# Eight rows of an expert product and a recurrence on one Trainium2 core: first-group weight sums through PSUM or put off, and a rewritten ending in quarters of 32 partitions

## The chip, the cores and the metric

The kernel runs on one core of one Trainium2 chip. A core has five engines that run their own queues of instructions: TensorE (PE; its weight loads are shown apart as PEld), VectorE (DVE), ScalarE (ACT), GpSimd (POOL) and SyncE (SP), which here issues the transfers. Work is passed between them by semaphores. SBUF and PSUM are the on-chip memories, both of 128 partitions; TensorE writes to PSUM only, in banks of 2 KB a partition (512 float32 columns). The metric is the device time of one execution in microseconds; lower is better.

## What is computed

The input x has 4 x 1024 tokens of width 1024, all in float32. Cut to what matters:

```python
xn  = layernorm(x)
# recurrence, batch 0 is enough (see below)
g   = sigmoid(xn @ gate_w.T + gate_b);  u_g = xn * g
d_eff = d + mean_over_tokens(u_g) @ d_lr_u @ d_lr_v / 4
s   = ...                       # first-order recurrence along the tokens, with a, b
y   = c * s + d_eff * u_g
# experts: indices are expert numbers 0..7, and they index rows of the output
p   = softmax(xn @ wr.T);  top 2 -> indices, gates
h   = silu(silu(xn @ w1.T) @ w3.T) @ w2.T
moe = zeros;  moe[indices[:, k]] += gates[:, k] * h      # k = 0, 1
out = x + y * silu(moe)
```

The scatter adds into rows 0 to 7 only, since there are eight experts. All other rows of moe are zero, silu(0) is zero, and these rows of the output are those of x. So the kernel copies x to out for all rows past the eighth, and computes eight rows: the sum over all 4096 tokens, C.T @ h2 with h2 = silu(silu(xn w1.T) w3.T) and C the 4096 x 8 matrix of gates, then (C.T @ h2) @ w2.T, then the last line. The gate g is needed for all tokens of batch 0, because of the mean; the recurrence is needed for eight tokens.

## The kernel before

**Groups and products.** The tokens are taken in four groups of 1024 (`sb` 0 to 3). For each group there are two 1024 x 1024 x 1024 products, `u` (xn with w1) and `m` (the result with w3); group 0 has a third, `g` (xn with gate_w), interleaved with `u`. Each is done with Strassen-Winograd's seven products in place of eight (`order` gives their order, by number 1 to 7) of 512 x 512 x 512, and each of those again with seven of 256 x 256 x 256, except some called plain, which use eight. A small product is four matmuls of 128 x 128 weights and 256 columns (`small`); the profile counts two records for each, so eight a small product. `Half` is one 512-product: `step(n)` issues its small product n, into the PSUM banks X, Z and Y, and drains them by `first` and `more`, on VectorE or ScalarE.

**The sums.** Strassen-Winograd needs sums of the operands' blocks. On the token side these are `s1` to `s4` (blocks) and `left_sums` (quarters of blocks); on the weight side the blocks 4 to 7 are differences of blocks of the weight (in `first_weights` for w1 and gate_w: `five`, `six`, `seven`, `four`; in `first_w3`: `take`), and `fresh_sums` and `t_sum` make four quarters of each (GpSimd). A block is 128 x 2048 values in SBUF, in four parts of 512 columns, so 1 MB; a quarter is 256 KB. There are 20 blocks and 18 quarters, handed out in turn. Group 0 makes the weight-side sums and stores them in HBM (`keep_block`, `keep_quarter`); groups 1 to 3 load them (`load_kept`, `load_kept_sum`). Plain products need no quarters, so group 0 makes those of w1 product 1 only to be kept (`kept_sums_1`), and group 1 makes those of w3 products 2 and 7 afresh.

**The order of the work.** `at(place, f)` puts a piece of work at a place of a written-out order; a small product of one half takes two places, and two halves overlap, so that a half adds 7 places (a plain one 8). `start[kind, sb, i]` is the place at which a product begins, END the place of the end. The loop over `steps` runs what is due and then the next small product. A generator's `yield n` puts its rest n places later. All instructions issued through `pe`, `dve`, `act`, `pool` and `sync` (all shown as L89, the line of the recording helper) stay in that order on their engine. SyncE's queue is in order too: a load behind a store that waits for its data waits as well.

**The other work that the change meets.** `stats` loads the rows of the next group and ScalarE sums them; `norm` normalizes the next group; `recurrence` makes y, [128, 8, 8] (width in 8 parts, 8 tokens).

**The end.** As soon as the two h2 blocks (I, 0) and (I, 1) of one token half I are complete, `scatter` issues eight matmuls of 32 weight columns (gates, padded from 8 to 32 columns) into the bank `acc`: column group g = 2 J + n % 2, so that the output's four sets of 32 partitions hold the two width halves J and, of each, two partial sums. The bank stays open over the whole program. The last `scatter` comes after the last product. Then the bank is copied, eight matmuls with `selh` (a selecting matrix) turn and add it to `ta`, 16 matmuls with w2 give `pp` in two banks, in four partial sums of 32 partitions each; for each half of 512 columns `pp` is copied, added up by a matmul with `sel` into 8 partitions, and goes through Silu, multiplication by y, addition of x and a store:

```python
    for n in range(2):
        cols = slice(n * H, (n + 1) * H)
        nc.vector.tensor_copy(ppS[:, cols], pp[n])
        ps = ps_x.tile([E, H], F32, tag="X", name=f"p2_{n}")
        nc.tensor.matmul(ps, sel, ppS[:, cols], start=True, stop=True)
        nc.scalar.activation(o8[:, cols], ps, AF.Silu)
        nc.vector.tensor_mul(o8[:, cols], o8[:, cols], y8[:, cols])
        nc.vector.tensor_add(o8[:, cols], o8[:, cols], x8[:, cols])
        nc.sync.dma_start(out[0:E, cols], o8[:, cols])
```

Of the kernel before, what the change touches and what calls it, by code (L numbers as in the profile page):

```python
# [22 lines left out]
def kernel(  # L23
# [113 lines left out]
    def quarter(uses=1):  # L137
# [13 lines left out]
    sel = const.tile([P, E], F32, tag="sel", name="sel")  # L151

    selh = const.tile([P, 2, E], F32, tag="selh", name="selh")
    nc.gpsimd.memset(selh, 0.0)
# [4 lines left out]
        sel, ident.rearrange("p (g e) -> p e g", e=CG)[:, 0:E, :], AX.X, ALU.add  # L159
    )  # L160
    dve.tensor_copy(ids, ids_i)
    for h in range(2):
        dve.tensor_copy(selh[64 * h : 64 * h + 64, h, :], sel[64 * h : 64 * h + 64, :])
# [7 lines left out]
    y = const.tile([P, KD, E], F32, tag="y", name="y")  # L171
# [315 lines left out]
    def fresh_sums(kind, sb, i, t, keep):  # L487
# [3 lines left out]
        for j in range(4):  # L491
# [6 lines left out]
            op_ts[kind, sb, i, j] = o  # L498
            if keep:
                at(start[kind, sb, i] + 2 * T_AT[j], keep_quarter, name, i, j, o)  # L500
# [4 lines left out]
    def sub(eng, out, p, q, n=4):  # L505

        for h in range(0, 4, 4 // n):
            eng.tensor_tensor(
                out[:, h : h + 4 // n], p[:, h : h + 4 // n], q[:, h : h + 4 // n], ALU.subtract
            )  # L510
            yield 0.5

    def load_kept(kind, sb, i, fresh):
        name = {"u": "w1", "m": "w3"}[kind]
        t = block(1 + fresh)
        sync.dma_start(t.tile, weights[name][raw[i]] if i in raw else kept[name, i])
        op_t[kind, sb, i] = t
# [6 lines left out]
    def first_weights(kind, name, before=()):  # L524
# [15 lines left out]
        def kept_sums_1():  # L540
            s = []
            for j in range(4):
                o = quarter(1 + (j < 2))
                t_sum(o, b[1], s, j)
                s.append(o)
                if j == 1:
                    s[0].drop()
                if j == 3:
                    s[1].drop()
                at(S(1) + 18 + 3 * j, keep_quarter, name, 1, j, o)  # L550
                yield 3
            b[1].drop()

# [10 lines left out]
        def six():  # L564
            yield from sub(dve, b[6], b[6], b[5])
# [13 lines left out]
        def four():  # L579
            yield from sub(pool, b[4], b[4], b[6])  # L580
# [9 lines left out]
        load(1, (0, 0), 2 + keep, before)  # L590
        one()
        if keep:
            at(S(1) + 8, kept_sums_1)
# [12 lines left out]
        for i in order["u"][1:]:  # L606
            if kind == "g" and i in PLAIN_G:
# [4 lines left out]
                lambda i=i: fresh_sums(kind, 0, i, op_t[kind, 0, i], keep),  # L612
            )

    def first_w3():
# [10 lines left out]
        def take(i, p=None, q=None):  # L626

            if p is not None:
                for h in range(4):
                    dve.tensor_tensor(b[i][:, h], b[p][:, h], b[q][:, h], ALU.subtract)  # L630
                    yield 1
# [15 lines left out]
        at(S(1) - 20, take, 5, 5, 1)  # L647
        at(S(1) - 12, take, 6, 6, 5)
# [633 lines left out]
```

## Time and profile before

| what | us |
|---|---|
| median of 3 runs | 851.44 (850.01 to 852.07) |
| the profiled execution | 850.65 |
| its span, first to last instruction | 848.6 |
| TensorE busy in the span | 831.2 |
| VectorE busy | 565.7 |
| GpSimd busy | 496.6 |
| ScalarE busy | 234.5 |
| mean granted TensorE clock | 0.997 of full |

The profile is of one execution; its times begin at the first instruction. A row of the timeline has the start, the length, the engine, the line, the operation, output and inputs by tile name, the shape, and in brackets how long the engine stood before it and who released it. A row of the groups has a count, the total busy time and the mean of one in nanoseconds. A row of the busy times by stretch has, for each engine, busy microseconds and the number of instructions that touch the stretch, then the granted clock, the share of the DMA engines in use, and GB/s. Matmuls overlap, so a busy TensorE is not one at its peak.

### The profile page before, as it was taken

What the parts mean: (1) busy time and instruction counts of PE and PEld (TensorE: products, weight loads), DVE (VectorE), ACT (ScalarE), POOL (GpSimd) and SP (SyncE); (2) the same over time, 40 slices, a digit from 0 to 9 for tenths busy, and PEclk for the clock granted to TensorE, in tenths of its full rate; (3) what the DMA queues carried; (4) which work ended last, traced back from release to release, by engine and by line L of the source; (5) the groups of instructions that cost most, each with busy time, mean ns of one, the idle gap of its engine ahead of it and who ended that gap; (6) DMA issues with size and microseconds to landing.
All of it is one profiled execution on the core that took longest, in us unless ns stands there. A gap on an engine that the chain in (4) does not pass through costs nothing.

```text
span 848.6 us, 11192 instructions
## 1 busy us (share of the span) xinstructions
PE 831.2 (98%) x4103; PEld 701.9 (83%) x4103; DVE 565.7 (67%) x889; ACT 234.5 (28%) x375; POOL 496.6 (59%) x375
## 2 busy tenths in 40 slices
PE   7999999989999999999999999999999999999997
PEld 6886888878888868888888778888888688888882
DVE  6989796988699425575897225775993246546642
ACT  0212213776121207343012226531122021220121
POOL 0389999995628764436866753753449444465400
PEclk9999999999999999999999999999999999999998
DMA  8953447631976877529976757659775455555600
GB/s 335 421 193 131 161 169 273 260 124 51 361 303 216 305 268 255 200 87 343 363 234 242 266 183 267 234 190 398 270 246 183 165 192 209 195 192 191 264 0 2
DMA packets 54013, 189.71 MB, mean 224 GB/s; under 512 B 6140, under 2 KB 9388, under 8 KB 42312
## 3 DMA queue, kind: packets, MB, share of 16 engines
q1 hardware_dynamic: 53960, 189.01, 60.2%
q8 instruction: 33, 0.54, 0.3%
q14 instruction: 20, 0.16, 0.1%
HBM read 165.86 MB, written 39.87 MB: 242 GB/s over the span
## 4 chain that ended last, share of the span: by engine, by line
PE 87%; DVE 7%; DMA 4%; SPq 1%; issue 1%; ACT 0%; DVEq 0%; ACTq 0%
PE X_u L89 21%; PE X_m L89 20%; PE Z_u L89 11%; PE Z_m L89 11%; DVE b L89 7%; PE Y_u L89 5%; PE X_g L89 5%; PE Y_m L89 4%; PE Z_g L89 3%; DMA b<-in_xT 3%; PE acc L89 2%; PE plT L89 2%; DMA b<-in_gw 1%; SPq L89 1%; PE Y_g L89 1%
## 5 line engine op out<-in xcount | busy, mean ns | idle before, releaser
L89 POOL TENSOR_TENSOR q<-b 128x512 f32<-128x512 f32 x144 | 202.8, 1421 | 230.6 <-DVE b L89 51.8
L89 ACT ACTIVATE b<-b 128x512 f32<-128x512 f32 (+1 forms) x152 | 105.0, 695 | 331.2 <-DVE b L89 322.1
L89 DVE TENSOR_TENSOR b<-b,b 128x512 f32<-128x512 f32 x176 | 181.8, 1052 | 3.3 <-POOL q L89 0.5
L89 POOL TENSOR_TENSOR q<-b,q 128x512 f32<-128x512 f32 x91 | 132.1, 1454 | 5.7 <-issue 3.3
L89 POOL TENSOR_TENSOR b<-b,b 128x512 f32<-128x512 f32 x72 | 94.5, 1336 | 40.5 <-PE X_u L89 34.4
L89 DVE TENSOR_TENSOR b<-X_u,b 128x512 f32<-128x512 f32 x87 | 59.9, 689 | 71.4 <-PE X_u L89 70.8
L89 PE MATMUL X_u<-q,q 128*128 128x256 f32 x432 | 103.1, 381 | 0.9 <-DVE b L89 0.9
L89 DVE TENSOR_TENSOR b<-X_m,b 128x512 f32<-128x512 f32 x84 | 57.2, 687 | 62.3 <-PE X_m L89 61.0
L89 PE MATMUL X_m<-q,q 128*128 128x256 f32 x416 | 98.3, 379 | 0.0
L89 PEld LDWEIGHTS X_u<-q,q 128*128 128x128 f32 x432 | 81.1, 190 | 16.1 <-issue 3.0
L89 POOL TENSOR_TENSOR q<-q,b 128x512 f32<-128x512 f32 x53 | 72.5, 1368 | 30.3 <-PE X_u L89 26.2
L89 PEld LDWEIGHTS X_m<-q,q 128*128 128x128 f32 x416 | 79.0, 190 | 10.8
L89 DVE TENSOR_TENSOR b<-b,bc 128x1024 f32<-128x1024 f32 (+1 forms) x62 | 72.8, 1178 | 3.6 <-ACT bc L89 2.5
L89 PE MATMUL X_m<-b,b 128*128 128x256 f32 x272 | 63.7, 380 | 0.9 <-DVE b L89 0.9
L89 PE MATMUL X_u<-b,b 128*128 128x256 f32 x248 | 58.8, 381 | 5.7 <-DVE b L89 5.5
L89 PEld LDWEIGHTS X_m<-b,b 128*128 128x128 f32 x272 | 51.3, 190 | 8.9 <-DVE b L89 1.9
L89 PEld LDWEIGHTS X_u<-b,b 128*128 128x128 f32 x248 | 46.8, 190 | 13.5 <-DVE b L89 6.7
L89 DVE TENSOR_TENSOR b<-Z_u,b 128x512 f32<-128x512 f32 x47 | 32.4, 689 | 28.6 <-PE Z_u L89 28.0
L89 PE MATMUL X_u<-b,q 128*128 128x256 f32 x216 | 51.3, 380 | 0.0
L89 PE MATMUL Y_u<-b,b 128*128 128x256 f32 x216 | 51.3, 380 | 0.0
L89 PE MATMUL Z_u<-q,b 128*128 128x256 f32 x216 | 51.3, 380 | 0.0
L89 DVE TENSOR_TENSOR b<-Z_m,b 128x512 f32<-128x512 f32 x48 | 32.8, 686 | 27.5 <-PE Z_m L89 26.1
(143 smaller groups left out, 1171.5 us busy)
## 6 DMA issues: line engine op xcount, KB each, us to landing
q<-w SPq DMA_DIRECT2D x160, 256.0 KB, 3.3
b<-in_w SPq DMA_DIRECT2D x35, 1024.0 KB, 7.4
b<-w_T SPq DMA_DIRECT2D x24, 1024.0 KB, 5.1
b<-in_xT SPq DMA_DIRECT2D x15, 1024.0 KB, 9.5
w<-q SPq DMA_DIRECT2D x56, 256.0 KB, 5.6
b<-in_x SPq DMA_DIRECT2D x12, 1024.0 KB, 7.3
w_T<-b SPq DMA_DIRECT2D x8, 1024.0 KB, 4.1
b<-in_gw SPq DMA_DIRECT2D x7, 1024.0 KB, 10.2
```

What stands on the lines that cost most here:

```text
L89: r = f(*args, **kwargs)
```

## The change

In group 0 the differences `six` and `four` of w1 and gate_w (sums of SBUF operands on VectorE and on GpSimd) are made by `with_bank`: ScalarE copies one operand, quarter by quarter, to one of two PSUM banks (`acc` and the bank of `rows`), and VectorE subtracts it from there. The quarters to be kept of w1 product 1 are no longer made in group 0's first stage, but by `late_sums` in its w3 stage, from a block that is read again; those of w3 products 2 and 7 are made by `late_sums` in group 1's u stage, so that group 1's m stage loads them as every other. In `first_w3`, takes 7 and 4 go to GpSimd, and takes 5 and 6 begin two places later.

At the end the scatter of the last group is cut in three: blocks (0,0) and (1,1) shortly after the last product has begun, (1,0) before its last but one small product, and the last block, (0,1), in a bank of its own, `accB`, in two halves. The rest of the sum is transposed and added in the meantime (`most`); `the_rest` then runs the product with w2 in pieces, as parts of its left side come in. The result is made as four quarters of 256 columns on 32 partitions each, with y and x laid out in the same way by `rows` 40 places before the end, and stored with four transfers from two queues.

```diff
-    selh = const.tile([P, 2, E], F32, tag="selh", name="selh")
-    nc.gpsimd.memset(selh, 0.0)
-    y = const.tile([P, KD, E], F32, tag="y", name="y")
+    y = const.tile([P, KD, CG], F32, tag="y", name="y")
+    pool.memset(y, 0.0)
...
+    def with_bank(out, p, q):
+        def copy(j):
+            spare[0] += 1
+            ps = acc if spare[0] % 2 else ps_acc.tile([P, H], F32, tag="rows", name="spare")
+            act.copy(ps, q[:, j])
+            return ps
+        ps = copy(0)
+        yield 0.5
+        for j in range(4):
+            ahead = copy(j + 1) if j < 3 else None
+            dve.tensor_tensor(out[:, j], p[:, j], ps, ALU.subtract)
+            ps = ahead
+            yield 0.5
+    def late_sums(name, i):
+        t = block()
+        sync.dma_start(t.tile, weights[name][raw[i]] if i in raw else kept[name, i])
+        yield 5
+        s = []
+        for j in range(4):
+            o = quarter(1 + (j < 2))
+            t_sum(o, t, s, j)
...
+            yield 2.5
+            keep_quarter(name, i, j, o)
+        t.drop()
...
-        def kept_sums_1():
...
         def six():
-            yield from sub(dve, b[6], b[6], b[5])
+            yield from with_bank(b[6], b[6], b[5])
...
         def four():
-            yield from sub(pool, b[4], b[4], b[6])
+            yield from with_bank(b[4], b[4], b[6])
...
         def take(i, p=None, q=None):
-                for h in range(4):
-                    dve.tensor_tensor(b[i][:, h], b[p][:, h], b[q][:, h], ALU.subtract)
-                    yield 1
+                yield from sub(pool if i in (7, 4) else dve, b[i], b[p], b[q], 4, 1)
...
-        at(S(1) - 20, take, 5, 5, 1)
-        at(S(1) - 12, take, 6, 6, 5)
+        at(S(1) - 18, take, 5, 5, 1)
+        at(S(1) - 10, take, 6, 6, 5)
...
-            fresh = kind == "m" and sb == 1 and i in PLAIN_M
-            at(S - (12 if fresh else 10), load_kept, kind, sb, i, fresh)
-            if fresh:
-                at(
-                    S - 5,
-                    lambda i=i: fresh_sums("m", 1, i, op_t["m", 1, i], True),
-                )
-            for j in range(0 if fresh else 4):
+            at(S - 10, load_kept, kind, sb, i)
+            for j in range(4):
                 at(S + 2 * T_AT[j] - 9, load_kept_sum, kind, sb, i, j)
...
+    at(start["m", 0, 1] + 14, late_sums, "w1", 1)
+    for n, i in enumerate(PLAIN_M):
+        at(start["u", 1, 1] + 4 + 14 * n, late_sums, "w3", i)
...
+    def rows():
+        end = block()
+        yR, xR = end[:, 0, 0:Q], end[:, 0, Q : 2 * Q]
+        pool.memset(xR, 0.0)
+        for w in range(4):
+            sync.dma_start(xR[CG * w : CG * w + E, :], x[0:E, w * Q : (w + 1) * Q])
+        yield 2
+        ty = ps_sm.tile([P, 2, P], F32, tag="sm", name="ty")
+        for j in range(2):
+            for w in range(4):
+                pe.matmul(ty[CG * w : CG * (w + 1), j, :], y[:, 2 * w + j, :], ident, ...)
+        yield 1
+        dve.tensor_copy(yR, ty.rearrange("e j p -> e (j p)"))
...
+    def most():
+        accs = fin["accs"]
+        act.copy(accs[:, Q:H], acc[:, Q:H])
+        dve.tensor_copy(accs[:, 0:Q], acc[:, 0:Q])
+        yield 2
+        tT = ps_sm.tile([P, 4, P], F32, tag="sm", name="tT")
+        for k in range(4):
+            pe.transpose(tT[:, k, :], accs[:, k * P : (k + 1) * P], ident)
+        yield 1
+        half = fin["half"] = fin["half"].rearrange("p (k e) -> p k e", e=E)
+        for J, o in ((0, fin["accT"][:, 0:4, 0:E]), (1, half)):
+            dve.tensor_copy(o, tT[:, :, 64 * J : 64 * J + E])
+            dve.tensor_add(o, o, tT[:, :, 64 * J + CG : 64 * J + CG + E])
+    def part_out(ks, start, stop):
+        for g, k in enumerate(ks):
+            for n in range(2):
+                r = (g + 2 * n) % 4 * CG
+                pe.matmul(fin["p"][n][r : r + CG, :], fin["accT"][:, k, :],
+                    w2_sb[n, k // 4][:, k % 4, :], ...)
+    def the_rest():
...
+        def last_block(b):
+            for n in range(4):
+                a, mt = n // 2, n % 2
+                pe.matmul(accB[n * CG : (n + 1) * CG, b * Q : (b + 1) * Q],
+                    gates[NS - 1][:, n, :], c[:, 2 * a + b, mt * Q : (mt + 1) * Q], ...)
+        last_block(1)
+        dve.tensor_copy(accBs[:, Q:H], accB[:, Q:H])
+        part_out(range(4), True, False)
+        ta = ps_sm.tile([P, 4, E], F32, tag="sm", name="ta")
+        for b in (1, 0):
+            ks = slice(2 * b, 2 * b + 2)
+            if b == 0:
+                dve.tensor_copy(accBs[:, 0:Q], accB[:, 0:Q])
+            for k in (2 * b, 2 * b + 1):
+                pe.matmul(ta[:, k, :], accBs[:, k * P : (k + 1) * P], sel[:, 0:E], ...)
+            if b == 1:
+                last_block(0)
+            dve.tensor_add(accT[:, 4 + 2 * b : 6 + 2 * b, 0:E], ta[:, ks, :], half[:, ks, :])
+            part_out((4 + 2 * b, 5 + 2 * b), False, b == 0)
+        for n, copy in ((0, dve.tensor_copy), (1, act.copy)):
+            copy(pp[:, n * H : (n + 1) * H], fin["p"][n])
+        p2 = ps_y.tile([P, Q], F32, tag="Y", name="p2")
+        for w in range(4):
+            pe.matmul(p2[CG * w : CG * (w + 1), :], sel, pp[:, w * Q : (w + 1) * Q], ...)
+        act.activation(o, p2, AF.Silu)
+        dve.tensor_mul(o, o, fin["y"])
+        dve.tensor_add(o, o, fin["x"])
+        for w in range(4):
+            (sync, act)[w % 2].dma_start(out[0:E, w * Q : (w + 1) * Q], o[CG * w : CG * w + E, :])
+    at(END - 40, rows)
+    at(start["m", NS - 1, 7] + 15, scatter, NS - 1, [(0, 0), (1, 1)])
+    at(END + 1.5, scatter, NS - 1, [(1, 0)])
+    at(END + 1.6, most)
+    at(END + 6, the_rest)
```

What is removed at the end is the old ending: the transposes of y to 8 partitions, the copies of `acc`, `ta`, `pp` and the loop quoted above.

## The prediction

> **What bounds the kernel now.** The page's busy table comes first. TensorE is busy for 98% of the span, so only time in which it stands, or the stretch after its last large product, can be won.
>
> ```profile
> PE 831.2 (98%) x4103; PEld 701.9 (83%) x4103; DVE 565.7 (67%) x889; ACT 234.5 (28%) x375; POOL 496.6 (59%) x375
> ```
>
> The timeline of TensorE alone shows where it stands (the bracket: idle time before, and who ended it). Past the first 17 us there are five holes; the fifth is 0.29 us at 368.39.
>
> ```profile
> 69.39 1.99 PE L89 MATMUL X_u<-b,b 128*128 128x256 f32 x8 [1.59 <-DVE b L89]
> ...
> 161.94 1.97 PE L89 MATMUL X_u<-q,q 128*128 128x256 f32 x8 [0.94 <-DVE b L89]
> ...
> 174.91 1.99 PE L89 MATMUL X_u<-b,b 128*128 128x256 f32 x8 [2.36 <-DVE b L89]
> ...
> 430.10 1.99 PE L89 MATMUL X_m<-b,b 128*128 128x256 f32 x8 [0.92 <-DVE b L89]
> ```
>
> Together 1.59 + 0.94 + 2.36 + 0.92 + 0.29 = 6.1 us. The first four end with VectorE, which drains the bank that the next product writes. The busy time by stretch (columns: PE, weight load, VectorE, ScalarE, GpSimd, clock, DMA share, GB/s) says why VectorE is late: in the first group GpSimd has no rest either.
>
> ```profile
> 67.00:102.00 35.00, 33.41 (x198) 26.20 (x197) 31.24 (x60) 9.50 (x17) 35.00 (x26) 1.00 0.38 143
> 102.00:150.00 48.00, 48.00 (x224) 42.27 (x223) 39.37 (x52) 11.20 (x19) 46.58 (x32) 1.00 0.62 234
> 150.00:186.00 36.00, 32.70 (x150) 28.17 (x150) 33.15 (x43) 26.54 (x37) 36.00 (x24) 1.00 0.46 179
> ```
>
> And the groups say what the two do to each other: one VectorE sum of two SBUF operands costs 1,052 ns in the mean, one with an operand in PSUM 689.
>
> ```profile
> L89 DVE TENSOR_TENSOR b<-b,b 128x512 f32<-128x512 f32 x176 | 181.8, 1052 | 3.3 <-POOL q L89 0.5
> ...
> L89 POOL TENSOR_TENSOR b<-b,b 128x512 f32<-128x512 f32 x72 | 94.5, 1336 | 40.5 <-PE X_u L89 34.4
> L89 DVE TENSOR_TENSOR b<-X_u,b 128x512 f32<-128x512 f32 x87 | 59.9, 689 | 71.4 <-PE X_u L89 70.8
> ```
>
> Last, the timeline of the end. The last large product is issued out at 830.77 (828.77 + 1.99), the span ends at 848.6: 17.8 us of chain.
>
> ```profile
> 828.77 1.99 PE L89 MATMUL X_m<-q,b 128*128 128x256 f32 x8
> ...
> 831.13 2.14 PE L89 MATMUL acc<-b,C 128*32 128x512 f32 x16
> ...
> 833.81 1.96 PE L1184 MATMUL ta<-selh,b 128*128 128x8 f32 x16 [0.54 <-DVE b L1177]
> ...
> 836.09 5.34 PE L1191 MATMUL pp<-b,accT 128*32 128x512 f32 x32 [0.32 <-DVE accT L1185]
> ...
> 842.35 0.59 ACT L1203 ACTIVATE b<-p 8x512 f32<-8x512 f32 x1 [8.14 <-PE p L1202]
> ...
> 845.00 0.68 DVE L1205 TENSOR_TENSOR b<-b,b 8x512 f32<-8x512 f32 x1
> ```
>
> **The change, part one: the first group.**
> (a) six, for u and g: 8 VectorE sums of SBUF operands become 8 ScalarE copies into PSUM and 8 sums from PSUM. In the timeline at 71.57 six such sums took 9.56 us, 1.59 each; at 0.69 each the eight give VectorE back 8 x 0.9 = 7 us. ScalarE's copy between SBUF and PSUM is 0.56 to 0.59 (the copies of X_u and bc); it has 25 of 35 us free there. Behind the copies in ScalarE's queue stands the drain of X_u of product 5, which TensorE needs before the bank's next use 8 us later; four copies ahead of it, two of them waiting for VectorE, cost about 2.5 us, so it is covered. Without that cover TensorE would stand for the 2.5.
> (b) four, for u and g: 8 GpSimd sums x 1.34 = 10.7 us leave an engine with 1.4 free us in 102 to 150; VectorE gains 8 x 0.69 = 5.5 us where it has 8.6 free, ScalarE 8 x 0.58 = 4.6 where it has 37.
> (c) The four sums kept of w1 product 1, and their four stores, leave the stretch 29 to 50 (4 x 1.27 = 5 us of GpSimd); everything behind them, the eight subtractions of five included, comes up to 5 us earlier. These matter: at 54.63 one VectorE sum took 5.34 us while GpSimd ran seven of them back to back, and the 1.59 us hole is the backlog from it. The sums come back at about 210 with one more 1 MB load.
> (d) In the w3 stage of the first group takes 7 and 4 go from VectorE to GpSimd (8 x 1.34), takes 5 and 6 start two places later, behind the drains that TensorE waits for at 162 and 175. With (c) GpSimd gets 12 sums, 16 us, in 186 to 292, where it is busy for 64 of 106.
> (e) w3 products 2 and 7: 8 sums and 8 stores move from about 395 to 430 to about 290 to 340, where VectorE is busy for only 37 of 78 us (stretch 292 to 370) and GpSimd for 46; in their old place come 8 loads of 256 KB. Two 1 MB blocks are read twice.
>
> A rule of the Trainium skill speaks against (a) and (b): "VectorE: DVE Perf Modes", section on the TRN2 errata, gives VectorE a fixed 120 cycles for a PSUM source against 58 for SBUF. By it each moved sum would cost 62 cycles at 0.96 GHz, 0.06 us, more: 16 x 0.06 = 1 us lost, and the copies on top. The rows say the reverse, 0.69 against 1.05 (1.59 at 71.57), since here GpSimd runs beside it. I take the rows.
>
> What of the holes goes: the 1.59 fully (c takes away more than its length); of 0.94 + 2.36 two thirds, 2.2, since GpSimd arrives there with about 10 us less behind it, but 24 of its sums remain there; of 0.92 half, because the chain that ended last shows the load of the next group's x (386.9 to 409) ahead of it, which stays; the 0.29 stays. That is 4.3 us. For the two places that receive work I charge 0.5 us of new holes: 3.8 net. Bounds: 6.1, all holes gone, and -2, the moved work making holes of its own.
>
> Behind waits: the loads of the x rows (four instead of one, on SyncE 40 places before the end) now wait for a memset on GpSimd, which stands up to 5.6 us for TensorE; late_sums' stores on SyncE wait for their GpSimd sum. Behind them in the queue stand the weight loads. Those are issued 9 or 10 places ahead, a place being 1.73 us (one step of 8 records), so 15.5 us, and land in 3.3: some 12 us of cover. If it is gone, the excess is a hole.
>
> **Part two: the end.** Ahead of the last product there now lie the scatter of (0,0) and (1,1) (as long as the old one, 1.85; it replaces the one at 826.92), the scatter of (1,0) alone, and four transposes. (1,0) uses two of the four column groups, so its 8 records take as long as 16 in four groups: 1.7. A transpose costs one 128-column weight load, 0.12 (ta: 16 in 1.96): 4 x 0.12 = 0.5 here. Their ACT and VectorE copies lie under the product in between (1.73 against about 1.1). The y products move off the end to 40 places ahead and stay near 0.43. So the last product is out at 830.77 + 2.2 = 833.0; I take 832.8. From there, with TensorE at 0.107 us a record of 512 columns in four groups (the fast part of pp), VectorE 0.42 for 128x256 (the copy of acc at L1177), 0.69 for 128x512, 0.06 for a hand-over:
>
> last_block(1) 0.43; part_out of four blocks, 16 records, 1.75 (the copy of accB, 0.75 to 1.17, lies beside it); ta 0.5; last_block(0) 0.43 (the add of 0.2 beside it); part_out, 8 records, 0.87; ta 0.5; add with hand-overs 0.35; part_out 0.87; copies of pp 0.75 (two engines); p2 0.6; Silu 0.45; multiply and add 2 x 0.42; issue and landing. Sum up to the issue: 0.43 + 1.75 + 0.5 + 0.43 + 0.87 + 0.5 + 0.35 + 0.87 + 0.75 + 0.6 + 0.45 + 0.84 = 8.3, with gaps 8.5. Before, from the last add's end (845.68) to the span's end lie 2.9 us. Now each of two queues issues two stores; one issue is 0.30 on SyncE, so 3.2. A ScalarE store is in no row; between SyncE's 0.30 and the 0.46 of SyncE's first loads (1.83 for four), near the first. End: 832.8 + 8.5 + 3.2 = 844.5, that is 4.1 us earlier.
>
> In this sum the clock is full. That is a choice. Before, the granted clock fell in the middle of pp:
>
> ```profile
> 836.00:836.50 0.50, 0.41 (x4) 0.16 (x8) 0.03 (x1) 0.00 (x0) 0.00 (x0) 0.99 0.00 0
> 836.50:837.00 0.50, 0.50 (x8) 0.21 (x4) 0.00 (x0) 0.00 (x0) 0.00 (x0) 0.50 0.00 0
> ...
> 840.00:841.00 1.00, 1.00 (x16) 0.31 (x9) 0.12 (x1) 0.00 (x0) 0.00 (x0) 1.00 0.00 0
> ```
>
> 3.2 us at half rate, 1.6 us lost. The skill's "TensorE: Matmul & The Clock Gate", section on the clock gate, halves the clock after an idle window of about 3.4 us. By that rule neither version should be halved, as TensorE never stood that long; by the row, three us of 8-column products and short gaps (833.3 to 836.1) were enough. The new end has no such stretch: about 60% of any 3.4 us is 256- or 512-column products. Were it halved from the second ta on, the last part_out and p2 would cost 1.3 more; from the start of the chain, with all its products (0.43 + 1.75 + 0.43 + 0.87 + 0.87 + 0.43), 4.8.
>
> **Sum.** 848.6 - 3.8 - 4.1 = 840.7 span; the profiled execution took 850.65, 2.05 more than its span, so 842.7. The median of the runs shown is 851.44, 0.8 above that execution; I say 843.0.
>
> **Rivals.**
> *Only one part delivers* (0.25): VectorE's 5.5 us from (b) and waits for ScalarE keep the holes, or the end is eaten by half clock and hand-overs. For it: VectorE is busy for 39 of 48 and 33 of 36 us and loses little in (b). Against: most of its excess is the 1.05 to 1.59 where 0.69 is the price. 850.65 - 4.1 or - 3.8, so 846.7, 847.3 by the median.
> *Nothing* (0.05): new holes as long as the old, and a halved end: 851.
> *Slower* (0.07): GpSimd becomes the bound in the w3 stage of the first group. Its 12 added sums are 16.2 us; its idle 42 of 106 us are waits for TensorE at fixed places, so if none of the sums fits in them, all delay TensorE: 850.65 - 8 + 16 = 859. It decides once half of them, 8 us, does. Against: at 97% GpSimd load (102 to 150) TensorE stood for nothing.
> *More* (0.08): all holes go: 840.5.
> The main case has 0.55. Its own range: 841 to 845.5. With the one-part case the range is 840 to 848.2; faster by over 0.3% (2.6 us, what a measurement of this kernel can tell) has 0.88, the same 0.05, slower 0.07.
>
> **What would show it.** Holes at 69, 162 and 175 gone and at 430 halved; GpSimd below 90% in 102 to 150; the sums from PSUM at 0.69; no hole over 0.5 us in 205 to 340; last product to span's end about 11.7 us at clock 1.00. Wrong if VectorE's drains still come late at 162 and 175, SyncE holds loads behind a store, or the clock is halved in part_out.

## The result, and the profile after

The changed kernel takes 842.43 us (median of six, 841.33 to 843.24), the kernel before beside it 850.57 (849.43 to 852.07): a ratio of 0.9899, with a 95% interval of 0.9885 to 0.9912. The profiled execution took 842.43 us, its span is 840.7 us, and its mean granted clock is 1.00. The forecast was 840.7 us of span and 843.0 of time.

The busy table of the page (busy us, share of the span, instructions):

```profile
PE 828.3 (99%) x4119; PEld 701.0 (83%) x4119; DVE 547.2 (65%) x890; ACT 243.2 (29%) x391; POOL 490.6 (58%) x377
```

TensorE's timeline (start, length; the bracket is the idle time before and who ended it). Past 17 us these are all the holes there are:

```profile
170.50 1.99 PE L89 MATMUL X_u<-b,b 128*128 128x256 f32 x8 [0.99 <-DVE b L89]
...
242.50 5.42 PE L89 MATMUL X_m<-b,b 128*128 128x256 f32 x24 [0.83 <-POOL b L89]
...
365.06 1.96 PE L89 MATMUL X_u<-b,b 128*128 128x256 f32 x8 [0.29 <-issue]
```

Before there were five, 6.1 us together. Those at 69, 162 and 430 are gone, the one at 175 went from 2.36 to 0.99, and there is a new one of 0.83 (the bracket names GpSimd; e7 below looks at what it waits for): 2.1 us now, 4.0 less.

The busy time by stretch, with the columns of before (TensorE, weight load, VectorE, ScalarE, GpSimd, clock, DMA share, GB/s):

```profile
67.00:102.00 35.00, 35.00 (x206) 27.92 (x205) 21.08 (x56) 14.05 (x26) 34.62 (x28) 1.00 0.57 204
102.00:150.00 48.00, 48.00 (x224) 42.25 (x223) 42.25 (x60) 17.18 (x29) 35.82 (x24) 1.00 0.56 209
150.00:186.00 36.00, 35.01 (x163) 30.50 (x162) 30.95 (x44) 25.90 (x36) 33.33 (x22) 1.00 0.41 159
205.00:245.00 40.00, 39.17 (x182) 34.18 (x182) 27.27 (x36) 6.17 (x10) 35.70 (x27) 1.00 0.92 355
```

VectorE is busy for 21.1 us in the first stretch where it was 31.2, GpSimd for 35.8 of 48 in the second where it was 46.6. The fourth row is where the late sums went. Before, GpSimd was busy there for 21.6 us and the DMA engines for 0.80 of the time; now it is 35.7 and 0.92. The row of before:

```profile
205.00:245.00 40.00, 40.00 (x187) 35.22 (x186) 30.65 (x43) 8.14 (x14) 21.61 (x15) 1.00 0.80 307
```

The groups of the page, and with them the rows that the view of the tile `spare` has for one of the two banks (there the durations are minimum, median and maximum in ns):

```profile
L89 DVE TENSOR_TENSOR b<-b,b 128x512 f32<-128x512 f32 x160 | 156.5, 995 | 2.9
...
L89 POOL TENSOR_TENSOR b<-b,b 128x512 f32<-128x512 f32 x72 | 95.4, 1352 | 35.8 <-PE X_u L89 26.4
```

```profile
L89 ACT COPY spare<-b x8: 575/590/595, 67.4 to 131.2; 128x512 f32<-128x512 f32 x8
...
L89 DVE TENSOR_TENSOR b<-b,spare x8: 675/678/689, 68.1 to 132.4; 128x512 f32<-128x512 f32 x8
```

A sum with one operand in PSUM takes 0.678 us with hardly any spread, also in the stretch from 67 to 102 us, where GpSimd is busy for 34.6 of 35. The VectorE sums that stay in SBUF still average 0.995.

The end, in the timeline of TensorE, ScalarE, VectorE and the queues:

```profile
822.79 1.91 PE L89 MATMUL acc<-b,C 128*32 128x512 f32 x8
...
826.90 1.89 PE L89 MATMUL X_m<-q,b 128*128 128x256 f32 x8
...
829.18 1.90 PE L89 MATMUL pp<-b,accT 128*32 128x512 f32 x16
...
833.86 1.06 PE L89 MATMUL pp<-b,accT 128*32 128x512 f32 x8 [0.27 <-DVE accT L89]
...
835.72 0.64 PE L89 MATMUL p<-b,sel 128*32 128x256 f32 x8 [0.80 <-DVE b L89]
...
836.84 0.88 DVE L89 TENSOR_TENSOR b<-b 128x256 f32<-128x256 f32 x2 [1.18 <-ACT b L89]
...
837.75 0.66 SPq L89 DMA_DIRECT2D out<-b  x2
837.75 0.96 ACTq L89 DMA_DIRECT2D out<-b  x2
```

The last large product is out at 826.90 + 1.89 = 828.79, and the span ends 11.9 us later; before it was 17.8. All products in it run at full clock; the clock is at half only from 840.2 on, when TensorE has nothing left to do. From the end of the last add (836.84 + 0.88 = 837.72) to the span's end lie 2.98 us.

### The profile page after: what moved, and what is told of

Its sections match the earlier page's. It is cut to its first block, busy times and chain, and to the rows that moved or that the text cites. A ratio compares the mean times of both kernels' runs of the same rounds, so it can differ in the third digit from the quotient of the medians.

```text
span 840.7 us, 11288 instructions
## 1 busy us (share of the span) xinstructions
PE 828.3 (99%) x4119; PEld 701.0 (83%) x4119; DVE 547.2 (65%) x890; ACT 243.2 (29%) x391; POOL 490.6 (58%) x377
## 4 chain that ended last, share of the span: by engine, by line
PE 91%; DMA 4%; POOL 1%; DVE 1%; issue 1%; SPq 1%; ACT 0%; POOLq 0%; DVEq 0%
PE X_u L89 23%; PE X_m L89 20%; PE Z_u L89 12%; PE Z_m L89 11%; PE Y_u L89 6%; PE X_g L89 6%; PE Y_m L89 5%; PE Z_g L89 4%; PE acc L89 2%; PE plT L89 2%; DMA b<-in_w 2%; DMA b<-in_gw 1%; DVE b L89 1%; DMA w<-q 1%; POOL q L89 1%
## 5 line engine op out<-in xcount | busy, mean ns | idle before, releaser
L89 POOL TENSOR_TENSOR q<-b 128x512 f32<-128x512 f32 x144 | 198.5, 1391 | 229.5 <-DVE b L89 51.4
L89 DVE TENSOR_TENSOR b<-b,b 128x512 f32<-128x512 f32 x160 | 156.5, 995 | 2.9
L89 POOL TENSOR_TENSOR q<-b,q 128x512 f32<-128x512 f32 x91 | 129.6, 1427 | 8.8 <-issue 6.7
L89 POOL TENSOR_TENSOR b<-b,b 128x512 f32<-128x512 f32 x72 | 95.4, 1352 | 35.8 <-PE X_u L89 26.4
L89 PEld LDWEIGHTS X_u<-q,q 128*128 128x128 f32 x432 | 81.3, 190 | 14.9 <-POOL q L89 1.7
L89 PEld LDWEIGHTS X_u<-b,b 128*128 128x128 f32 x248 | 46.9, 190 | 10.2 <-DVE b L89 3.3
L89 PE MATMUL Z_u<-q,q 128*128 128x256 f32 x216 | 51.0, 379 | 0.0
```

Of the source, the lines that this page charges most:

```text
L89: r = f(*args, **kwargs)
```

## The experiments

Times are medians of the runs named; a ratio is to the kernel before on the same chip, with its 95% interval. The medians of before in these series are 851.36, 851.50, 850.76 and 851.34 us.

### One part at a time

**e1_end_only**: the kernel after with its first group put back as it was; only the new ending stays. The core of the edit, against the kernel after (the lines that e5 shows belong to it too):

```diff
-            yield from with_bank(b[6], b[6], b[5])
+            yield from sub(dve, b[6], b[6], b[5])
...
-            yield from with_bank(b[4], b[4], b[6])
+            yield from sub(pool, b[4], b[4], b[6])
...
-        load(1, (0, 0), 2, before)
+        load(1, (0, 0), 2 + keep, before)
         one()
+        if keep:
+            at(S(1) + 8, kept_sums_1)
...
-                yield from sub(pool if i in (7, 4) else dve, b[i], b[p], b[q], 4, 1)
+                yield from sub(dve, b[i], b[p], b[q], 4, 1)
...
-        at(S(1) - 18, take, 5, 5, 1)
-        at(S(1) - 10, take, 6, 6, 5)
+        at(S(1) - 20, take, 5, 5, 1)
+        at(S(1) - 12, take, 6, 6, 5)
...
-    at(start["m", 0, 1] + 14, late_sums, "w1", 1)
-    for n, i in enumerate(PLAIN_M):
-        at(start["u", 1, 1] + 4 + 14 * n, late_sums, "w3", i)
```

> The new ending alone, on the old first group. Theory (the two parts add up): the chain from the last large product to the span's end is about 11.9 us as in the changed kernel and the last product comes 2.2 us later for the work put ahead of it, so 850.6 - 3.7 to 4.1 = about 846.7; the holes at about 69, 162, 175 and 430 are all there again, 5.8 us. Rival (the first group's change is what made room for the new ending): the loads and copies of the ending come late and it is 848 or more. Rival (the ending did it all): 842.4.

Measured: 848.61 us over 19 runs (845.75 to 850.25), ratio 0.9967 [0.9959, 0.9975], which is 2.8 us less than before. In the profiled execution the chain behind the last product is 11.95 us (832.05 to 844.0): the ending is as short as in the kernel after. The gain is smaller than expected: by the interval it is 2.1 to 3.5 us, where 3.7 to 4.1 were forecast, and the time alone would fit the rival's 848. The runs lie widely apart; e11 below looks at that.

**e2_group_only**: the kernel after with the old ending.

```diff
-                if sb < NS - 1 and (I, 1 - J) in h2:
-                    at(here[0] + 6, scatter, sb, [(I, 0), (I, 1)])
+                if (I, 1 - J) in h2:
+                    at(here[0] + 6, scatter, sb, I)
...
-    at(END - 40, rows)
-    at(start["m", NS - 1, 7] + 15, scatter, NS - 1, [(0, 0), (1, 1)])
-    at(END + 1.5, scatter, NS - 1, [(1, 0)])
-    at(END + 1.6, most)
-    at(END + 6, the_rest)
...
     run_todo(10**9)
+    end = block()
...
+        nc.sync.dma_start(out[0:E, cols], o8[:, cols])
```

> The new first group alone, with the old ending. Theory: holes of 2.1 us in place of 6.1, so 850.6 - 4.0 = 846.6; the old ending takes 17.8 us from the last product with the clock at 0.50 for about 3 us of it. Rival (holes moved, not closed): 850.6. Rival (the half clock of the ending was an accident of that one execution): the clock stays at 1.00 and the ending takes about 16.2 us, 845.

Measured: 844.71 us (843.43 to 847.48, four runs), 0.9925 [0.9906, 0.9944], 6.4 us less than before. The profiled execution was the one at 847.48. Its holes are 1.00 at 172.69, 0.88 at 244.75 and 0.30 at 367.31, so the hole at 430 is gone there too; its end is 17.5 us long, and the clock halves in it as it did before:

```profile
833.56 5.34 PE L1209 MATMUL pp<-b,accT 128*32 128x512 f32 x32 [0.32 <-DVE accT L1203]
```

Both parts deliver, and -2.8 and -6.4 add up to -9.2 where the whole is -8.6 (1.0% of 851.4): they are independent within the intervals. But the halves stand otherwise than the forecast had them: 4.1 for the end lies above its interval (2.1 to 3.5), and 3.8 for the group below its own (4.8 to 8.0).

### What the PSUM operand is worth

**e3_no_bank**: without (a) and (b), the rest as after.

```diff
-            yield from with_bank(b[6], b[6], b[5])
+            yield from sub(dve, b[6], b[6], b[5])
...
-            yield from with_bank(b[4], b[4], b[6])
+            yield from sub(pool, b[4], b[4], b[6])
```

> The changed kernel with six back on VectorE and four back on GpSimd, both from SBUF; all else as changed. Theory: the hole at 69 stays closed (it is the kept sums that were put off), the holes at 162 and 175 come back for the most part, 2 us more than 0.99; GpSimd is above 95% busy in 102 to 150: about 844.5. Rival (the put-off sums alone closed all): 842.4. Rival (the PSUM operand did all): all holes back, 846.4.

Measured: 845.31 us (844.87 to 845.84), 0.9939 [0.9922, 0.9955]: 2.9 us over the kernel after by the medians, 3.4 by the ratios. The timeline has the two holes of before again, and none at 69:

```profile
160.49 1.97 PE L89 MATMUL X_u<-q,q 128*128 128x256 f32 x8 [0.94 <-DVE b L89]
173.01 1.99 PE L89 MATMUL X_u<-b,b 128*128 128x256 f32 x8 [1.92 <-DVE b L89]
```

So the hole at 162 and most of what went from the one at 175 go by (a) and (b): 1.87 us of 2.31 come back. That there is no hole at 69 says less here than in e4, as in this execution the clock was at half between 12.4 and 15.9 us, and such a stretch shortens that hole too (see the last section).

**e8_dve_sbuf**: the same sums on VectorE with both operands in SBUF. GpSimd is relieved of `four` as after, but nothing lies in PSUM.

```diff
-            yield from with_bank(b[6], b[6], b[5])
+            yield from sub(dve, b[6], b[6], b[5])
...
-            yield from with_bank(b[4], b[4], b[6])
+            yield from sub(dve, b[4], b[4], b[6])
```

> The changed kernel with six and four both on VectorE, but both from SBUF: GpSimd is relieved as in the change, only the PSUM operand is missing. Theory (the price of a sum is what GpSimd does beside it): the 16 sums take 1.0 to 1.6 us each in place of 0.68, 5 to 15 us more of VectorE in 66 to 150, and holes of 1 to 4 us come: 843.5 to 846.5. Rival (the relief of GpSimd was enough, and the PSUM copies buy nothing): 842.4, the sums at 0.69.

Measured: 847.45 us (846.09 to 849.67, six runs), 0.9959 [0.9944, 0.9973]: 5 us over the kernel after, and over e3 too. VectorE's and TensorE's timelines:

```profile
70.79 9.55 DVE L89 TENSOR_TENSOR b<-b,b 128x512 f32<-128x512 f32 x6
```

```profile
131.38 3.42 PE L89 MATMUL X_g<-b,b 128*128 128x256 f32 x8 [2.82 <-DVE b L89]
```

Six sums in SBUF again take 9.55 us, 1.59 each, where the view of `spare` after has 0.678; and VectorE, with the work of `four` added at 1.3 to 1.4 us a sum, makes a new hole of 2.82 us. The clock falls to half at 130.9 us, in that hole, and stays there until 134.3, so that the eight records behind it take 3.42 us instead of 1.99. To hand work of GpSimd to VectorE at the price of SBUF is a loss, 2.1 us against e3; the operand in PSUM is what makes room.

It is not that SBUF is slower by itself. In e6 below, GpSimd stands for 12.14 us up to 244.79, and a VectorE sum of two SBUF operands in that time takes as long as one from PSUM:

```profile
239.17 0.69 DVE L89 TENSOR_TENSOR b<-b,b 128x512 f32<-128x512 f32 x1
```

```profile
244.79 1.28 POOL L89 TENSOR_TENSOR q<-b 128x512 f32<-128x512 f32 x1 [12.14 <-DVE b L89]
```

So a busy GpSimd makes VectorE's sums of two SBUF operands longer, and leaves those with one operand in PSUM as they are.

### The sums put off

**e4_kept_early**: without (c). The four sums kept of w1 product 1 are made at their old place.

```diff
-        load(1, (0, 0), 2, before)
+        load(1, (0, 0), 2 + keep, before)
         one()
+        if keep:
+            at(S(1) + 8, kept_sums_1)
...
-    at(start["m", 0, 1] + 14, late_sums, "w1", 1)
```

> The changed kernel with the four kept sums of w1 product 1 back in the first stage. Theory: the hole at 69 comes back, 1.6 us; the one at 242.5 (0.83 us, new with the change) goes, since the block's second load is gone: 842.4 + 0.8 = 843.2. Rival (the PSUM operand is what closed the hole at 69): no hole there, 841.6.

Measured: 842.82 us (842.18 to 843.43), 0.9907 [0.9891, 0.9924], within the interval of the kernel after. The timeline:

```profile
69.07 1.99 PE L89 MATMUL X_u<-b,b 128*128 128x256 f32 x8 [1.61 <-DVE b L89]
...
172.06 1.99 PE L89 MATMUL X_u<-b,b 128*128 128x256 f32 x8 [1.01 <-DVE b L89]
```

There is no hole at 242. Both halves of the expectation hold: (c) is what closes the hole at 69 (1.61 us comes back), and it is what makes the one at 242.5 (0.83 goes). Half of what it wins it gives back, and the rest is too small for the medians to show.

**e7_late_34**: the late sums 20 places later, behind the takes of w3.

```diff
-    at(start["m", 0, 1] + 14, late_sums, "w1", 1)
+    at(start["m", 0, 1] + 34, late_sums, "w1", 1)
```

> The changed kernel with the put-off sums of w1 product 1 twenty places later (about 35 us), past the stretch in which the DMA engines are busy for 0.92 of the time. Theory (that block's second load delays the load of w3 block 4): the hole at 242.5 is gone, 841.6. Rival (the takes on GpSimd are too slow whatever the load): it stays, 842.4.

Measured: 842.18 us (840.96 to 843.78), 0.9901 [0.9884, 0.9917]. The profiled execution has a span of 839.2 us; its only holes are 1.00 at 170.06 and 0.28 at 363.54, and the one at 242.5 is gone. GpSimd's timeline, in the kernel after and then in this one, at take 4 (the bracket again names who ended the wait):

```profile
235.16 1.27 POOL L89 TENSOR_TENSOR b<-b,b 128x512 f32<-128x512 f32 x1 [2.38 <-DMA b<-in_w]
```

```profile
230.88 5.42 POOL L89 TENSOR_TENSOR b<-b,b 128x512 f32<-128x512 f32 x4 [2.83 <-DMA b<-in_w]
```

After, the load of the block of w3 that take 4 subtracts from is issued at 219.45, and the block is there at 235.16, 15.7 us later. With the late sums' own 1 MB load out of the way it comes 4.3 us earlier (0.4 of that is the whole timeline, which is ahead by so much from the start), and the four subtractions follow one another instead of standing between sums of w1. The DMA engines are as busy as before, 0.92 of 205 to 245. But in SyncE's queue everything behind the load moves up: the next load of x is issued at 211.90 instead of 214.40, and the first of the two row loads `q<-flat` at 221.44 instead of 224.35, which is 2 to 2.5 us beyond the 0.4 of the timeline.

What TensorE waits for at 242.50 is not take 4 itself, as the bracket has it: GpSimd's last sum of it ends at 237.62 + 4.19 = 241.81. It is VectorE's drain of X_m, which ends 0.1 us ahead of 242.50. VectorE in the kernel after:

```profile
237.12 1.22 DVE L89 TENSOR_TENSOR b<-b,bc 128x1024 f32<-128x1024 f32 x1 [3.19 <-ACT bc L89]
...
238.97 1.70 DVE L89 TENSOR_TENSOR b<-b,b 128x512 f32<-128x512 f32 x1
...
241.72 0.68 DVE L89 TENSOR_TENSOR b<-X_m,b 128x512 f32<-128x512 f32 x1
```

VectorE had stood for 3.19 us, until ScalarE had copied a row to `bc`, and the drains stand behind that in its queue. The copy comes at 236.50 after, where its bracket names GpSimd's first sum of take 4, which had itself waited for the late block, and at 233.65 in e7, where it waits for the load `q<-flat`. So the late transfers reach TensorE through VectorE's queue.

**e6_takes_dve**: takes 7 and 4 back on VectorE, the late sums where the change has them. This parts the load from the load on GpSimd.

```diff
-                yield from sub(pool if i in (7, 4) else dve, b[i], b[p], b[q], 4, 1)
+                yield from sub(dve, b[i], b[p], b[q], 4, 1)
```

> The changed kernel with takes 7 and 4 back on VectorE. Theory (the hole at 242.5 is the load of w3 block 4, which landed late and on which take 4 waited): it stays, 0.5 to 1 us, with VectorE as the one that ends it: 842.4. Rival (GpSimd's 12 added sums made it): it is gone, 841.6.

Measured: 843.01 us (841.76 to 843.44), 0.9903 [0.9886, 0.9919].

```profile
242.25 5.45 PE L89 MATMUL X_m<-b,b 128*128 128x256 f32 x24 [0.38 <-DVE b L89]
```

```profile
237.32 1.22 DVE L89 TENSOR_TENSOR b<-b,bc 128x1024 f32<-128x1024 f32 x1 [1.58 <-ACT bc L89]
...
241.51 0.68 DVE L89 TENSOR_TENSOR b<-X_m,b 128x512 f32<-128x512 f32 x1
```

With the takes on VectorE 0.38 of 0.83 is left. ScalarE's copy comes as late as before (236.69, and here it waits for `q<-flat`), so the late transfers are still there. What is gone is the sum of 1.70 us beside GpSimd's take 4; the sum in its place is the one of 0.69 shown above. So take 4 on GpSimd lengthens the hole, and without the late transfers there is none (e7). The time is the same within the interval.

**e5_w3_fresh**: without (e). Products 2 and 7 of w3 make their sums afresh in the second group, as before.

```diff
-            at(S - 10, load_kept, kind, sb, i)
-            for j in range(4):
+            fresh = kind == "m" and sb == 1 and i in PLAIN_M
+            at(S - (12 if fresh else 10), load_kept, kind, sb, i, fresh)
+            if fresh:
+                at(
+                    S - 5,
+                    lambda i=i: fresh_sums("m", i, op_t["m", 1, i], True, 1),
+                )
+            for j in range(0 if fresh else 4):
...
-    for n, i in enumerate(PLAIN_M):
-        at(start["u", 1, 1] + 4 + 14 * n, late_sums, "w3", i)
```

> The changed kernel with the sums of w3 products 2 and 7 back in group 1's w3 stage. Theory (the hole at 430 was GpSimd's fresh sums beside VectorE): 0.9 us there again, 843.3. Rival (it came from the late load of the next group's x): none, 842.4.

Measured: 844.18 us (843.44 to 845.22), 0.9915 [0.9899, 0.9932]. The holes are 1.01 at 172.53, 0.97 at 244.68 and 0.28 later; there is none at 430. The theory isn't borne out, but the trace doesn't refute it either. The drain that TensorE waits for there is late again, only less so (e5, and then e9, which has the old first group and the old (e)):

```profile
428.12 1.99 PE L89 MATMUL X_m<-b,b 128*128 128x256 f32 x8
```

```profile
429.19 1.99 PE L89 MATMUL X_m<-b,b 128*128 128x256 f32 x8
```

In both the product follows 0.1 us behind the end of the one before and 0.06 behind VectorE's drain of X_m. In the kernel before the same wait was 0.92, in the traces of e1 and e11, also with the old group, 0.76 and 1.17. So one and the same code has given 0.1 to 1.17 us, and one trace of e5 can't tell whether its 0.1 is due to the new first group or to chance. What it does show: with the old (e) GpSimd is busy for 18.0 of the 20 us from 410 to 430 (18.2 before, 10.1 after), and VectorE works without a pause up to this drain, while in the kernel after the drain is done at 424.86, 0.8 us ahead of its product (425.70). The time is 1.7 us over the kernel after by the medians, with intervals that overlap, and the profiled execution began with half clock from 11 to 18 us, so that it isn't shown that (e) is worth anything.

### The ending

**e9_gate_fill**: the kernel before, with one dummy product of 256 columns ahead of each product of `ta`. Nothing uses what they write.

```diff
+    fill = ps_sm.tile([P, Q], F32, tag="sm", name="fill")
+    def filler():
+        nc.tensor.matmul(fill, ones, w2_sb[0, 0][:, 0, 0:Q], start=True, stop=True, skip_group_check=True)
+    filler()
     for k in range(KD):
+        if k:
+            filler()
```

> The kernel before, with eight dummy products of 256 columns (their output is not used) put between and ahead of the eight-column ones of ta, so that TensorE streams densely there. Theory (thin products and gaps count as idle for the clock): the clock stays at 1.00 to the end; pp takes 3.7 us in place of 5.34, while ta grows by about 3. Rival (the clock falls at that point of the program whatever the stream): 0.50 again in pp, 5.3 us.

Measured, one execution with its profile: 850.78 us.

```profile
838.02 3.64 PE L1201 MATMUL pp<-b,accT 128*32 128x512 f32 x32 [0.32 <-DVE accT L1195]
```

The same 32 records took 5.34 us before. The clock stayed at 1.00 until TensorE's last product, which points to the thin stretch of 8-column products as what halves it in the traces of before and e2. It is one execution, and the old ending doesn't halve the clock every time: one of the four of e2 has a mean clock of 0.999, which leaves room for a loss of 1.3 us at most, less than the 1.7 of pp. The fillers cost about 3 us for the 1.7 that they save, so they are no gain.

**e10_one_queue**: the four stores of the result on one queue.

```diff
-            (sync, act)[w % 2].dma_start(
+            sync.dma_start(
```

> The changed kernel with all four result stores issued by SyncE. Theory: two more issues of 0.3 us each behind one another, so from the last add's end to the span's end 3.6 us in place of 3.0. Rival (the stores' landing sets the end, whoever issues): 3.0.

Measured, one execution with its profile: 843.07 us, span 841.3.

```profile
837.92 1.33 SPq L89 DMA_DIRECT2D out<-b  x4
```

The last add ends at 837.89, and the span 3.4 us later, against 2.98 with two queues in the kernel after. The other traces with two queues have 2.9 to 3.0, but e6 has 3.3. So the second queue seems to save 0.4 us, but that rests on one execution, and those with two queues differ by as much among themselves.

**e11_end_only_2**: e1 once more, for a second trace of it, as e1's profiled execution was its fastest. The edit is that of e1.

> The new ending alone once more, for a second trace: its median lay 2.8 us below the kernel before where the sum said 3.7, and its executions spread over 4.5 us. Theory (the old first group's hole at 69 and the half clock at about 11 to 18, which some executions have, trade against each other): with full clock at the start the hole at 69 is 1.6 us, the others as in the first trace. Rival (the new ending holds up loads): a hole past 740, or weights that land late there.

Measured, one execution with its profile: 849.25 us, span 847.5.

```profile
69.35 1.99 PE L89 MATMUL X_u<-b,b 128*128 128x256 f32 x8 [0.54 <-DVE b L89]
...
174.90 2.42 PE L89 MATMUL X_u<-b,b 128*128 128x256 f32 x8 [2.37 <-DVE b L89]
...
432.08 1.99 PE L89 MATMUL X_m<-b,b 128*128 128x256 f32 x8 [1.17 <-DVE b L89]
```

There is no hole past 740 us, so the rival, that the new ending's loads hold up the weights, fell. The chain behind the last product is again 12.0 us (835.54 to 847.5). What is longer lies far ahead of the ending: half clock from 12 to 16 us, where the first 16 records of X_u take 5.38 us instead of 3.72, half clock once more from 176.3 to 179.7, behind the hole of 2.37, and a longer hole at 430.

### A better version

**e12_late_34_warm**: e7 with five dummy products in the lull at the start (8 to 12.4 us), in which TensorE runs only short products. Nothing uses what they write.

```diff
             )
+            if (I, a) == (0, 0):
+                for _ in range((2, 3)[s]):
+                    pe.matmul(idle, ones, ident, start=True, stop=True, skip_group_check=True)
...
-    at(start["m", 0, 1] + 14, late_sums, "w1", 1)
+    at(start["m", 0, 1] + 34, late_sums, "w1", 1)
```

> The changed kernel with the put-off sums twenty places later, and five dummy products of 128 columns (their output is not used) in the gaps of TensorE between 8.9 and 12.4. Theory (those gaps let the clock fall to half at about 11 in some executions, up to 6 us of it): the clock stays at 1.00 in 10 to 20 in every execution, so the median is 1 to 1.5 us below the version without the dummies, about 841.0, and no execution is above 842. Rival (the gaps have nothing to do with it[...]): the same executions with half clock, 842.2.

Measured: 841.41 us (841.10 to 841.72, four runs), 0.9884 [0.9868, 0.9901].

```profile
12.39 3.72 PE L89 MATMUL X_u<-b,b 128*128 128x256 f32 x16 [0.83 <-DVE b L89]
...
170.43 2.00 PE L89 MATMUL X_u<-b,b 128*128 128x256 f32 x8 [0.98 <-DVE b L89]
```

It is the fastest of all by its median, and its four runs lie within 0.6 us where e7's lie within 2.8. Its interval overlaps with those of e7 and of the kernel after, so that it beats before is shown, and that it beats the kernel after is not.

## Why the prediction was right

The span was forecast at 840.7 us and is 840.7. That the two agree to 0.1 us is luck, as the executions of the kernel after differ by 1.9 us; that the holes and the chain at the end are what was won is not. By its steps:

- **Holes, 3.8 net forecast, 4.0 found.** The 1.59 at 69 was to go by (c), and e4 shows that it does. Of 0.94 + 2.36 two thirds, 2.2, were to go by (a) and (b); 0.94 + 1.37 = 2.3 went, and without (a) and (b) 1.9 of them come back (e3). The size of the step was the room that (a) gives VectorE: 7 us were forecast, and in 67 to 102 it has 10.2 more (31.24 to 21.08), of which 9.0 are (a)'s and (b)'s (30.05 in e3).
- **The operand in PSUM.** The forecast took 0.69 from a row against the price of the Trainium skill's "VectorE: DVE Perf Modes", section on the TRN2 errata, by which a PSUM source is the dearer one. Measured: 0.678 from PSUM, 0.69 from SBUF while GpSimd stands (e6), 1.59 from SBUF beside it (e8). The page's 62 cycles more, 0.06 us, are not seen in either comparison, and the row decides.
- **The hole at 430 is the weakest step.** Half of it was to go by (e). All of it went, 0.46 us more than forecast, but e5 doesn't show that (e) did it, and in e9 it is all but absent with nothing of the change there. With the old group it was in three traces of four, with the new one in none; what sets its length stays open.
- **New holes, 0.5 forecast, 0.83 found.** "No hole over 0.5 us in 205 to 340" was wrong. The working said that weight loads land in 3.3 us and so have 12 us of cover. That is the mis-sized term. 3.3 is the median of the quarters of 256 KB (`q<-w`) in the page of before; its blocks of 1 MB (`b<-in_w`) have 7.4, and in 205 to 245, with the DMA engines busy for 0.92 of the time, one took 15.7. The forecast named (c)'s additional 1 MB load, but not that it holds up what is issued behind it. Nor did it see the path: the wait goes through the row loads, ScalarE's copy and VectorE's queue. e7 removes the hole by moving these sums; e6 shows that take 4 on GpSimd makes it longer, so (d) and (c) meet there. The rows of the page of before (KB each, median us from issue to landing):

```profile
q<-w SPq DMA_DIRECT2D x160, 256.0 KB, 3.3
b<-in_w SPq DMA_DIRECT2D x35, 1024.0 KB, 7.4
```

- **GpSimd as the bound, the slower rival.** GpSimd rose to 35.7 of 40 us in 205 to 245, and TensorE lost 0.83 us, not 16. Nearly all of its added sums fitted into its waits.
- **The end, 4.1 forecast.** Without the holes the last product would be out at 828.79 + 4.0 = 832.8, as forecast: the scatter of (1,0) and the transposes cost their 2.2 (the eight records of two column groups took 1.91 where 1.7 was said). From there 8.93 us to the issue (8.5 forecast) and 2.98 (3.2 forecast): 11.9 for 11.7. Between them the two traces give 17.8 - 11.9 - 2.0 = 3.9 us for this part.
- **The clock.** Full clock in the new end was a choice, and held. By the rule of the Trainium skill's "TensorE: Matmul & The Clock Gate", section on the clock gate (an idle window of about 3.4 us), the old end would not have been halved, by its row it was, and the row decides; e9 speaks for the row's reading, three us of thin products, and e8 has half clock from 2.3 us after the beginning of a hole of 2.82.

By medians the account is less neat. The end alone is worth 2.8 us where 4.1 were forecast, the group alone 6.4 where 3.8 were, and both forecasts lie outside the intervals. The two errors have opposite signs, and that their sum comes out right is in part luck.

The clock has a share in this. The mean granted clock of each execution is known, in steps of 0.001, so the time at half clock can be taken off: the median over a kernel's executions of its time less (1 - clock) x span. It is a coarse estimate. A step is 0.85 us, and half clock at the very end, when TensorE has nothing left to do, is taken off too (0.9 us in the trace of before, 0.25 in the one of after).

| kernel | median us | mean clock | us less the clock's part |
|---|---|---|---|
| before (38 executions, beside e1 to e8, e11 and e12) | 851.3 | 0.9946 | 846.1 |
| e1, end only | 848.6 | 0.9957 | 844.8 |
| e2, group only | 844.7 | 0.9962 | 842.0 |
| after | 842.4 | 0.9980 | 840.5 |

Of the 8.9 us between the first row and the last some 3 go with the clock in this estimate: 0.0034 x 849 = 2.9. The forecast counted 1.6, in pp. Of the rest the two traces show 0.7, the idle end; the remainder is in executions of which no trace was kept. At equal clock the group wins 4.1, as its holes say (4.0). The end wins 1.3 where 3.9 - 1.6 = 2.3 would be expected. With means in place of medians it is 1.9, so how much is missing isn't clear; the longer hole at 430 in e11 (1.17 for 0.92) is a part of it, and the rest stays unexplained. Whether the old first group meets half clock more often than the new one isn't settled either: no run changed only that.

## What to carry to other kernels

Where VectorE and GpSimd sum side by side, price an operation by the row that has the same neighbours and not by its shape: there a copy into PSUM on a ScalarE with time to spare brought VectorE's sums from 1.05 to 1.59 us down to 0.68. A sum that is put off takes its load with it, and in a stretch where the DMA engines are busy for 0.92 of the time that load holds up what is issued behind it (by 2 to 2.5 us for 1 MB here); look for who waits for those transfers, and don't count on a median landing time. When a bracket names an engine that had long been done, look at who ended just before. A chain of many small steps at the end is worth splitting so that only the last block's part is left behind the last large product; here it also left no stretch of thin products in which the clock fell.

## What was not expected of the hardware

The clock halves at the start in some executions and not in others of one and the same kernel. The stretch from 12 to 16 us (columns as above), after in its profiled execution, and then e2 in its own:

```profile
12.00:16.00 4.00, 3.57 (x16) 2.96 (x16) 3.93 (x8) 0.00 (x0) 0.00 (x0) 1.00 1.02 424
```

```profile
12.00:16.00 4.00, 3.55 (x8) 2.86 (x9) 3.93 (x8) 0.00 (x0) 0.00 (x0) 0.50 1.02 418
```

At half clock only eight records fit where sixteen did. It follows the lull from 8 to 12.4 us, in which TensorE has only short products, begins between 11.3 and 12.9 us and ends between 14.9 and 18.3. It is in the traces of e1, e2, e3, e5, e6, e8, e9 and e11, but not in those of before, after, e4, e7 and e10. With dummy products in the lull (e12) the clock of all four runs is 0.998 or more; that they are the reason is likely by e9, but not shown, as other versions have such runs without them.

Seen in steps of 0.1 us, half clock ahead of TensorE's last product comes in pieces of one length: 3.4 us in pp of before (836.5 to 839.9), at the start of e1, e3, e6, e9 and e11, behind the hole of 2.82 in e8 and behind the one of 2.37 in e11, and 6.8 us, twice that, at the start of e2, e5 and e8. So one piece costs up to 1.7 us. Holes of 2.36 and 2.37 at the same place in before, e1 and e9 brought none.

Half clock at the start also gives VectorE time to work off its backlog: with the old sums at the start, the hole at 69 was 1.59 and 1.61 in the traces of before and e4, which had full clock, 0.54 and 0.49 in those of e11 and e9, and there was none in that of e1. So a hole and a slow stretch ahead of it trade against one another, and neither is worth its full length.
